# Moving the second block of attention values, a projection and the out-projections to other score tiles in a one-core AdaLN block

## The chip, the cores and the metric

The kernel runs on one core of one Trainium2 chip. The metric is the device time of one execution in microseconds. The matrix engine is called PE or TensorE here, with PEld for its weight loads; VectorE is DVE, ScalarE is ACT, GpSimd is POOL, and SP is the engine whose queue issues most of the DMAs.

## What is computed

A transformer block with adaptive layer norm, in float32. There are B = 2 sequences of S = 1024 positions with D = 256 features, H = 16 heads of 128, and a gated MLP with 704 hidden units whose weights come as integers with a scale per row.

```
sa, ca, ga, sb, cb, gb = six rows of silu(c) @ wmod, per sequence
ga, gb = sign(g) * max(|g|, 0.25)
h = layernorm(x) * (1 + ca) + sa
q, k, v = h @ Wq + bq, h @ Wk + bk, h @ Wv + bv         # 16 heads
q, k = rotary(q / sqrt(128)), rotary(k)
p = softmax(causal(q @ k.T));  x = x + ga * (concat(p @ v) @ Wo + bo)
h = layernorm(x) * (1 + cb) + sb
x = x + gb * ((silu(h @ Wgate.T) * (h @ Wup.T)) @ Wdown.T)
```

## The kernel before, in words

The work is a list of 32 units, one for each sequence and head, called heads here and counted from 0 (in the code `units`, and `n` is the number in the list). Each head has eight score tiles `i` = 0 to 7 of 128 queries. Every engine works its instructions off in the order in which the Python code issues them: a manual schedule writes that order out by hand, so the place of a call in the loop (L733 to L773) is the place of its instructions in every queue, DMAs included. Pools of PSUM banks and of SBUF buffers add the waits: a new tile in a pool waits until the oldest one in it has been read.

One step of the loop, for head `n` and tile `i`, issues in this order:

- `project_out` (L511): two matmul instructions (each float32 product is two instructions) of an earlier head's output tile with `Wo` into the one bank of `ps_y`, and on VectorE the product with 1/denominator added to `x` (L521). Heads n-1 (tiles 0 to 3, at i = 4 to 7) and n-2 (tiles 4 to 7, at i = 0 to 3) take turns.
- `score` (L419): q times k for the causal part of 128(i+1) keys into one of the two buffers of `ps_sc`, then on VectorE the mask and the row minimum (L434).
- `turned` (L461): for tile i-1 VectorE transposes the probabilities in 32x32 pieces (L465) into a staging tile; after tiles 3 and 7 sixteen DMAs on SP (L477) finish the transposition of a block of four tiles into `pT`. Tile 7 is turned in tile 0 of the next head. Each block has one `pT` buffer.
- `expo` (L446): the exponential on ScalarE (L451), with the row sum.
- `release` (L414): VectorE's part of the rotary embedding (L404) for the last q or k projection, and GpSimd's addition (L407).
- `project_qk` (L379): half of the next head's q or k into one of the two banks of `ps_a`, with two ScalarE copies (L400) and a GpSimd product (L401). It is called at i = 1, 3, 4 and 6.
- `values` (L481): p times v for one block of 512 queries into the one bank `po` of `ps_o`, then a copy of it on ScalarE (L500). The second block of the previous head is at i = 5 and 6, four key tiles each; the first block of the head itself at i = 7.
- `project_v` (L362) at i = 0 and 2, into `ps_a`, and the scattered work of `extras` (L629): weight scaling, layer-norm statistics, the bias row (L347) and the modulation (L117).

In the last head there is no next head to project, and `hidden` (L534) for the first half of sequence 0 takes that place at i = 0 to 5: gate and up products (L547), SiLU on ScalarE (L566, or L558 for the last, narrower chunk) and the product on VectorE (L567, L562). Behind the loop (L775 to L808) the remaining gate and up chunks alternate with the remaining out-projections, which take a bank in turn from `banks` (L502); then come the last values, layer norm, and the down products (L569).

Of the kernel before, what the change touches and what calls it, by code (L numbers as in the profile page):

```python
# [13 lines left out]
AF = mybir.ActivationFunctionType  # L14
ALU = mybir.AluOpType
# [5 lines left out]
HID = 704  # L21
NT = S // P
# [3 lines left out]
NF = (HID + P - 1) // P  # L26
FULL = (HID // P) * P
# [10 lines left out]
def adaln_block(ctx: ExitStack, tc: tile.TileContext, a, cos_d, sin_d, out):  # L38
    nc = tc.nc
# [7 lines left out]
    ps_a = pool("ps_a", 2, space=PSUM)  # L47
    ps_o = pool("ps_o", 1, space=PSUM)
    ps_y = pool("ps_y", 1, space=PSUM)
# [94 lines left out]
    pgs = []  # L144
# [211 lines left out]
    def add_bias(b, t):  # L356
        nc.gpsimd.tensor_tensor(x[b][:, t, :], x[b][:, t, :], gbo[b], ALU.add)
# [123 lines left out]
    def values(u, blk, k0, k1):  # L481
        b, g, h = u
        if blk == 0 and k0 == 0:
            outs[u] = opool.tile([P, S], F32, tag="o", name=f"o_{b}{g}{h}")
        if k0 == 0:
            pos[u, blk] = ps_o.tile([P, 512], F32, tag="o", name=f"po_{b}{g}{h}{blk}")
        po = pos[u, blk]
        last = 4 * blk + 3
        pT = pTs[u, blk].rearrange("p r i k b -> p i r k b")
        for k in range(k0, k1):  # L490
            off = max(0, k - 4 * blk)
            nc.tensor.matmul(  # L492
                po[:, off * P :],
                vs[b, g][:, k, ts(h, DH)],
                pT[:, off:, :, k, :],
                start=(k == 0),
                stop=(k == last),
            )
        if k1 == last + 1:
            nc.scalar.copy(outs[u][:, ts(blk, QB)], po)  # L500

    banks = [(ps_y, "y"), (ps_o, "o"), (ps_a, "a"), (ps_a, "a")]  # L502
    turn = [0]

    def bank(name):
# [5 lines left out]
    def project_out(u, t, late=False):  # L511

        b, g, h = u
        if t % 4 == 0:
            nc.vector.reciprocal(rdens[u][:, t : t + 4], dens[u][:, t : t + 4])  # L515
        name = f"py_{b}{g}{h}{t}"
        py = bank(name) if late else ps_y.tile([P, 512], F32, tag="y", name=name)
        nc.tensor.matmul(  # L518
            py[:, :D], outs[u][:, ts(t, P)], weights[b, g]["o"][:, h, :], start=True, stop=True
        )  # L520
        nc.vector.scalar_tensor_tensor(  # L521
            x[b][:, t, :], py[:, :D], rdens[u][:, t : t + 1], x[b][:, t, :], ALU.mult, ALU.add
        )


    h2s, gTs = {}, {}
# [4 lines left out]
        h2s[b, blk] = hpool.tile([P, KC, QB], F32, tag=tag, name=f"h2_{b}{blk}")  # L531
        return h2s[b, blk]

    def hidden(b, blk, c, late=True, first=None):  # L534
        if c == 0 if first is None else first:
            gTs[b, blk] = fpool.tile([P, NF, QB], F32, tag="f", name=f"gT_{b}{blk}")
        last = c == NF - 1
        if late:
            pg = ps_sc.tile([P, S], F32, tag="sc", name=f"pgu_{b}{blk}{c}")
            pgs = [pg[:, ts(j, QB)] for j in range(2)]  # L540
        else:
            pgs = [
                ps_a.tile([P, 512], F32, tag="a", name=f"pgu_{b}{blk}{c}{j}") for j in range(2 - last)
            ]
        for pg, n in zip(pgs, ("gate",) if last else ("gate", "up")):
            for k in range(KC):
                nc.tensor.matmul(  # L547
                    pg,
                    wT["last"][:, k, :] if last else wT[n][:, k, ts(c, P)],
                    h2s[b, blk][:, k, :],  # L550
                    start=(k == 0),
                    stop=(k == KC - 1),
                )
        sg = ppool.tile([P, QB], F32, tag="p", name=f"sg_{b}{blk}{c}")
        if last:

            m = HID - FULL
            nc.scalar.activation(sg[m:], pgs[0][:m], AF.Silu)  # L558

            for j, rows_ in enumerate((slice(0, m), slice(m, P))):  # L560
                part = lambda t: t.rearrange("p (t j q) -> p t j q", j=2, q=P)[:, :, j, :]
                nc.vector.tensor_tensor(  # L562
                    part(gTs[b, blk][rows_, c, :]), part(sg[m:]), part(pgs[0][m:]), ALU.mult
                )
        else:
            nc.scalar.activation(sg, pgs[0], AF.Silu)  # L566
            nc.vector.tensor_tensor(gTs[b, blk][:, c, :], sg, pgs[1], ALU.mult)  # L567

    def down(b, blk):  # L569

# [58 lines left out]
    def extras(n, i):  # L629

        if i == (2 if n else 7) and units[n][2] == 0:
            fold_out(*units[n][:2])
        if n == 1 and i == 0:
            modulation(2, ps_y, "y")
            shift_scale(2)

        if n == 2 and i == 7:
            ffn_scale_load()
        for m, name in ((3, "gate"), (5, "up"), (6, "last")):
            if n == m and i == 7:  # L640
                ffn_weight_load(name)
            if n == m + 1 and i in (2, 5):
                ffn_weight_scale(name, i // 4)
        if n in (0, 4, 6, 8) and i == 7:
            load_x(1, max(0, n - 2), 2, nc.scalar)
        if n == 7 and i == 7:
            ffn_down_load()
        if n in (8, 9) and i in (1, 3, 5):
            ffn_down_scale(n - 8, i - 1)


        for m, b, name in ((14, 1, "a"), (30, 0, "b")):

            j = i - 1 if n in (m - 5, m - 3) else i + 3
            if n in (m - 5, m - 4) and 1 <= i <= 4:
                ln_stats(b, name, j)
            if n == m - 4 and i == 6:
                ln_sqrt(b, name, 0, NT)
            if n in (m - 3, m - 2) and 2 <= i <= 5:
                ln_move(b, name, j - 1)  # L660
            if n in (m - 3, m - 2) and 1 <= i <= 4:
                ln_scale(b, name, j // 4, (j % 4,))
            if n in (m - 2, m - 1) and i == 6:
                ln_send(b, name, ((0, 1), (2, 3))[n - m + 2])
            if n == m and i in (4, 5, 7):
                blk = i // 6
                if i != 5:
                    dest = (new_hT if b else new_h2)(b, blk)
                else:
                    dest = (hT if b else h2s)[b, blk]  # L670
                for f in {4: (0,), 5: (1,), 7: (0, 1)}[i]:
                    ln_shift(b, name, blk, 0 if b else 2, dest, f)
        if n == 14 and i == 5:
            bias_row()
        if n == 15:
            add_bias(0, i)
        if n == 20:
            add_bias(1, i)

    with tc.manual_schedule():  # L680
        pc = ps_a.tile([P, 512], F32, tag="a", name="pc")
# [51 lines left out]
        for n, u in enumerate(units):  # L733
            b, g, h = u
            prev = units[n - 1] if n else None
            nxt = units[n + 1] if n + 1 < N else None
            nb, ng = (b, g + 1) if g + 1 < NG else (b + 1, 0)
            more = nb < B
            for i in range(NT):

                if i < 4 and n > 1:
                    project_out(units[n - 2], 4 + i)
                if i >= 4 and prev:
                    project_out(prev, i - 4)
                ps, nmax = score(u, i)
                if i >= 1:
                    turned(u, i - 1)
                elif prev:
                    turned(prev, NT - 1)
                expo(u, i, ps, nmax)  # L750
                release()
                if i in (1, 3, 4, 6) and nxt:
                    project_qk(nxt, *{1: ("q", 0), 3: ("k", 0), 4: ("q", 1), 6: ("k", 1)}[i])
                if i in (5, 6) and prev:
                    values(prev, 1, 4 * (i - 5), 4 * (i - 4))

                if i == 7 and prev:
                    values(u, 0, 0, 4)
                if i in (0, 2):
                    if h == 0:  # L760
                        project_v(b, g, 4 + i, *((ps_a, "a") if n else (ps_o, "o")))
                    elif more:
                        project_v(nb, ng, i)
                if n == 1 and i == 2:
                    values(prev, 0, 0, 4)
                if not nxt and i < NF:
                    hidden(0, 0, i, late=False)
                extras(n, i)
                if i == 7 and h == 1:
                    if more:  # L770
                        load_out(nb, ng)
                    if n + 3 < N:
                        load_proj(*units[n + 3][:2])  # L773

        u, prev = units[-1], units[-2]  # L775
        turned(u, 7)
        for c in range(4):
            hidden(0, 1, c)
            project_out(prev, 4 + c, late=True)
            project_out(u, c, late=True)  # L780

        for t in range(4):
            ln_stats(1, "b", t)
# [91 lines left out]
```

## Time and profile before

| what | us |
|---|---|
| median of three runs (lowest, highest) | 1077.45 (1077.07, 1077.51) |
| the profiled execution, its own time | 1076.87 |
| its span, from first to last instruction | 1075.1 |
| TensorE matmul busy | 1068.8 |
| VectorE busy | 656.8 |
| ScalarE busy | 507.2 |
| GpSimd busy | 397.1 |
| ScalarE waiting for VectorE's row minimum (L451 for L434) | 406.8 |
| VectorE waiting for the scores (L434 for L431) | 124.5 |
| SP's queue waiting for VectorE's transposes (L477 for L465) | 236.6 |

The granted TensorE clock is 1.000 over the whole span. Two more lines of the page show what the queue of SP carries:

```profile
pT<-t SPq DMA_DIRECT2D x512, 128.0 KB, 2.4
pT<-t SPq DMA_DIRECT2D x512, 64.0 KB, 2.0
```

The last column is the median time from issue to landing in us. In the trace these DMAs are issued some 0.63 us apart, so sixteen of them take about 10 us of the queue.

A group's row in the profile gives line, engine, operation, the tiles written and read, the shape and the count; behind the bar stand the busy time and the mean length of one in ns; behind the second bar the engine's idle time just before them, with what ended it. In a timeline or a chain the columns are the start in us from the span's beginning, the length in us, and what ran. Each line of the chain follows what released the step before it.

### The profile page before, as it was taken

How to read it: one execution, taken by the hardware profiler on the slowest of the kernel's cores; microseconds unless marked ns; L12 is line 12 of the kernel's file. 1: busy time of each engine (PE TensorE's matmuls, PEld its weight loads, DVE VectorE, ACT ScalarE, POOL GpSimd, SP SyncE). 2: the span in 40 equal slices, each digit the busy share in tenths (PEclk: the TensorE clock that was granted, in tenths of full speed). 3: DMA queues.
4: the chain of work that ended last, by engine and by line, in shares of the span. 5: the costliest groups of instructions: out<-in, count | busy, mean ns of one | idle time of the engine just before them, and what ended most of it. 6: DMA issues, size and time to landing. Idle time of an engine off the chain costs nothing.

```text
span 1075.1 us, 12365 instructions
## 1 busy us (share of the span) xinstructions
PE 1068.8 (99%) x3529; PEld 639.0 (59%) x3529; DVE 656.8 (61%) x1423; ACT 507.2 (47%) x956; POOL 397.1 (37%) x364
## 2 busy tenths in 40 slices
PE   9999999999999999999999999999999999999998
PEld 5655556566666656556566666656556566555656
DVE  5666566767767766556666566666667856444421
ACT  4644445445445544445455444544455455562110
POOL 4725353535344343664343444334343434200000
PEclk9999999999999999999999999999999999999999
DMA  6455655657554556556564645454655556423001
GB/s 218 109 133 123 161 138 128 172 126 182 117 145 99 140 119 152 126 130 144 111 147 108 147 107 138 95 143 103 157 118 120 143 130 141 104 52 66 20 20 39
DMA packets 66655, 130.97 MB, mean 122 GB/s; under 512 B 18806, under 2 KB 22010, under 8 KB 66588
## 3 DMA queue, kind: packets, MB, share of 16 engines
q1 hardware_dynamic: 64804, 125.78, 49.5%
q10 hardware_dynamic: 1736, 4.29, 1.2%
q8 instruction: 28, 0.46, 0.2%
q14 instruction: 39, 0.32, 0.1%
q0 software_dynamic: 48, 0.13, 0.1%
HBM read 25.26 MB, written 2.10 MB: 25 GB/s over the span
## 4 chain that ended last, share of the span: by engine, by line
PE 98%; DMA 1%; ACT 0%; issue 0%; DVE 0%; SPq 0%; DVEq 0%; ACTq 0%
PE po L492 23%; PE ps L431 23%; PE pv L370 10%; PE pq L388 10%; PE pk L388 10%; PE py L518 10%; PE pgu L547 7%; PE pd L592 3%; DMA wmod<-in_wmod 0%; PE pd L582 0%; PE pm L125 0%; PE ptx_a L218 0%; ACT L566 0%; DMA pT<-t 0%; PE pg L149 0%; PE ptx_b L218 0%
## 5 line engine op out<-in xcount | busy, mean ns | idle before, releaser
L451 ACT ACTIVATE p<-ps,nmax 128x128 f32<-128x128 f32 (+7 forms) x256 | 189.6, 741 | 407.6 <-DVE nmax L434 406.8
L431 PE MATMUL ps<-kT,qT 128*128 128x512 f32 (+3 forms) x768 | 289.4, 486 | 0.0
L434 DVE CUSTOM_DVE_ANT_0 ps<-ps,mask 128x128 f32<-128x128 f32 (+7 forms) x256 | 195.4, 763 | 125.2 <-PE ps L431 124.5
L492 PE MATMUL po<-pT,v 128*128 128x512 f32 (+3 forms) x768 | 263.8, 486 | 0.7 <-DMA pT<-t 0.5
L521 DVE SCALAR_TENSOR_TENSOR x<-py,rden,x 128x256 f32<-128x256 f32 x256 | 122.8, 482 | 183.8 <-PE py L518 176.1
L492 PEld LDWEIGHTS po<-pT,v 128*128 128x128 f32 x768 | 145.4, 190 | 130.6 <-issue 107.5
L465 DVE STREAM_TRANSPOSE t<-p 128x128 f32<-128x128 f32 (+7 forms) x256 | 198.0, 773 | 3.0 <-DMA pT<-t 2.1
L431 PEld LDWEIGHTS ps<-kT,qT 128*128 128x128 f32 x768 | 145.7, 190 | 77.5 <-issue 64.3
L401 POOL TENSOR_TENSOR r_k<-r_k,sin_t 128x512 f32<-128x512 f32 x64 | 81.3, 1271 | 221.6 <-ACT r_k L400 221.5
L518 PE MATMUL py<-wo,o 128*128 128x256 f32 x512 | 151.3, 379 | 0.0
L407 POOL TENSOR_TENSOR kT<-kT,r_k 128x512 f32<-128x512 f32 x64 | 81.2, 1269 | 138.7 <-DVE rden L515 117.4
L401 POOL TENSOR_TENSOR r_q<-r_q,sin_t 128x512 f32<-128x512 f32 x64 | 81.6, 1275 | 137.0 <-ACT r_q L400 134.9
L518 PEld LDWEIGHTS py<-wo,o 128*128 128x128 f32 x512 | 92.6, 190 | 65.1 <-issue 53.1
L370 PE MATMUL pv<-wv,hT 128*128 128x256 f32 x512 | 121.1, 379 | 0.0
L388 PE MATMUL pq<-hT,wq 128*128 128x512 f32 x256 | 120.5, 593 | 0.0
L388 PE MATMUL pk<-hT,wk 128*128 128x512 f32 x256 | 120.3, 592 | 0.0
L370 PEld LDWEIGHTS pv<-wv,hT 128*128 128x128 f32 x512 | 94.8, 190 | 19.5 <-issue 1.3
L400 ACT ACTIVATE r_q<-pq,cols 64x512 f32<-64x512 f32 x128 | 87.3, 682 | 22.5 <-PE pq L388 20.2
L407 POOL TENSOR_TENSOR qT<-qT,r_q 128x512 f32<-128x512 f32 x64 | 83.5, 1305 | 32.2 <-DVE qT L404 29.4
L400 ACT ACTIVATE r_k<-pk,cols 64x512 f32<-64x512 f32 x128 | 87.3, 682 | 6.1 <-PE pk L388 0.4
L388 PEld LDWEIGHTS pk<-hT,wk 128*128 128x128 f32 x256 | 48.6, 190 | 54.6 <-issue 44.7
L388 PEld LDWEIGHTS pq<-hT,wq 128*128 128x128 f32 x256 | 46.2, 190 | 33.1 <-issue 30.6
(96 smaller groups left out, 686.9 us busy)
## 6 DMA issues: line engine op xcount, KB each, us to landing
pT<-t SPq DMA_DIRECT2D x512, 128.0 KB, 2.4
pT<-t SPq DMA_DIRECT2D x512, 64.0 KB, 2.0
wq<-in_Wq SPq DMA_DIRECT2D x16, 256.0 KB, 3.0
wk<-in_Wk SPq DMA_DIRECT2D x16, 256.0 KB, 4.1
wv<-in_Wv SPq DMA_DIRECT2D x16, 256.0 KB, 4.1
wo<-in_Wo SPq DMA_DIRECT2D x16, 256.0 KB, 2.9
out<-yo SPq DMA_DIRECT2D x15, 128.0 KB, 1.8
wmod<-in_wmod SPq DMA_DIRECT2D x4, 256.0 KB, 5.7
```

The lines of the kernel that those rows point to most:

```text
L370: nc.tensor.matmul(pv[:, ts(j, HG * DH)], hT[b, n][:, k, ts(r, P)], weights[b, g]["v"][:, k, :], start=(k == 0), stop=(k == KC - 1),)
L388: nc.tensor.matmul(pq, weights[b, g][s][:, k, ts(h, DH)], hT[b, n][:, k, :], start=(k == 0), stop=(k == KC - 1),)
L400: nc.scalar.activation(r1[to], pq[of], AF.Identity, bias=cols[of, c : c + 1])
L401: nc.gpsimd.tensor_tensor(r1, r1, sin_t[:, sl], ALU.mult)
L407: nc.gpsimd.tensor_tensor(dst[:, sl], dst[:, sl], r1, ALU.add)
L431: nc.tensor.matmul(ps[:, c:e], qT[:, ts(i, P)], kT[:, c:e], start=True, stop=True)
L434: nc.vector.tensor_tensor_reduce(ps[:, :L], ps[:, :L], mask[:, NT - 1 - i :, :].rearrange("p t k -> p (t k)"), -SCALE, FLT_MAX, ALU.add, A ...
L451: nc.scalar.activation(p[:, :L], ps[:, :L], AF.Exp, bias=nmax, scale=-1.0, accum_out=dens[u][:, i : i + 1])
L465: nc.vector.transpose(t32[blk][:, :, j, : i + 1, :].rearrange("p c k b -> p k c b"), p[:, : (i + 1) * P].rearrange("p (k c a) -> p k c a", ...
L492: nc.tensor.matmul(po[:, off * P :], vs[b, g][:, k, ts(h, DH)], pT[:, off:, :, k, :], start=(k == 0), stop=(k == last),)
L518: nc.tensor.matmul(py[:, :D], outs[u][:, ts(t, P)], weights[b, g]["o"][:, h, :], start=True, stop=True)
L521: nc.vector.scalar_tensor_tensor(x[b][:, t, :], py[:, :D], rdens[u][:, t : t + 1], x[b][:, t, :], ALU.mult, ALU.add)
```

## The change

Nothing is added to the computation and nothing is taken from it. These calls move:

- `values` of the previous head's second block: from tiles 5 and 6 to tiles 6 and 7.
- `values` of the first block: from tile 7 of the head itself to tile 0 of the next head, after `project_v` (tile 2 in head 1, as before). For the last head it goes behind the loop.
- `project_qk` for the second half of k: from tile 6 to tile 5.
- `project_out`: every one a tile later, now by a running number `s`.
- `hidden` in the last head: at tiles 0, 1, 3, 4, 5, 6; its product on VectorE is held back (`owed`) until after the next `project_out`, also behind the loop.
- the second modulation from head 1, tile 0 to head 0, tile 7; the bias row in head 14 from tile 5 to tile 7; the order of `banks`.

```diff
-    banks = [(ps_y, "y"), (ps_o, "o"), (ps_a, "a"), (ps_a, "a")]
+    banks = [(ps_y, "y"), (ps_a, "a"), (ps_a, "a"), (ps_o, "o")]
...
-    def hidden(b, blk, c, late=True, first=None):
+    def hidden(b, blk, c, late=True, first=None, hold=False):
...
+        rest = (last_gate_up if last else full_gate_up)(b, blk, c, sg, pgs)
+        if hold:
+            owed.append(rest)
+        else:
+            rest()
...
+    def full_gate_up(b, blk, c, sg, pgs):
+        nc.scalar.activation(sg, pgs[0], AF.Silu)
+        return lambda: nc.vector.tensor_tensor(gTs[b, blk][:, c, :], sg, pgs[1], ALU.mult)
...
-        if n == 1 and i == 0:
+        if n == 0 and i == 7:
             modulation(2, ps_y, "y")
             shift_scale(2)
...
-        if n == 14 and i == 5:
+        if n == 14 and i == 7:
             bias_row()
...
+    filler = (0, 1, 3, 4, 5, 6)
+
+    def shared_out(s, late=False):
+        if s >= 0:
+            project_out(units[s // NT], s % NT, late)
...
-                if i < 4 and n > 1:
-                    project_out(units[n - 2], 4 + i)
-                if i >= 4 and prev:
-                    project_out(prev, i - 4)
+                shared_out(8 * n + i - 13)
+                if owed:
+                    owed.pop()()
...
-                if i in (1, 3, 4, 6) and nxt:
-                    project_qk(nxt, *{1: ("q", 0), 3: ("k", 0), 4: ("q", 1), 6: ("k", 1)}[i])
-                if i in (5, 6) and prev:
-                    values(prev, 1, 4 * (i - 5), 4 * (i - 4))
-
-                if i == 7 and prev:
-                    values(u, 0, 0, 4)
+                if i in (1, 3, 4, 5) and nxt:
+                    project_qk(nxt, *{1: ("q", 0), 3: ("k", 0), 4: ("q", 1), 5: ("k", 1)}[i])
+                if i in (6, 7) and prev:
+                    values(prev, 1, 4 * (i - 6), 4 * (i - 5))
...
-                if n == 1 and i == 2:
+                if not nxt and i in filler:
+                    hidden(0, 0, filler.index(i), late=False, hold=True)
+
+                if prev and i == (0 if n > 1 else 2):
                     values(prev, 0, 0, 4)
-                if not nxt and i < NF:
-                    hidden(0, 0, i, late=False)
...
-        u, prev = units[-1], units[-2]
+        u = units[-1]
         turned(u, 7)
+        s = 8 * N - 13
         for c in range(4):
-            hidden(0, 1, c)
-            project_out(prev, 4 + c, late=True)
-            project_out(u, c, late=True)
+            hidden(0, 1, c, hold=True)
+            if c == 0:
+                values(u, 0, 0, 4)
+            for _ in range(2 + (c == 3)):
+                shared_out(s, late=True)
+                s += 1
+            owed.pop()()
```

More of the change, by code (lines that the diff above doesn't have):

```diff
@@ L554, in hidden, with last_gate_up, rest @@
         sg = ppool.tile([P, QB], F32, tag="p", name=f"sg_{b}{blk}{c}")
-        if last:
-            m = HID - FULL
-            nc.scalar.activation(sg[m:], pgs[0][:m], AF.Silu)
+        rest = (last_gate_up if last else full_gate_up)(b, blk, c, sg, pgs)
[3 more added lines that the diff above has]
+            rest()
+    owed = []
+    def last_gate_up(b, blk, c, sg, pgs):
+        m = HID - FULL
+        nc.scalar.activation(sg[m:], pgs[0][:m], AF.Silu)
+        def rest():
             for j, rows_ in enumerate((slice(0, m), slice(m, P))):
@@ L564, in hidden @@
                 )
-        else:
-            nc.scalar.activation(sg, pgs[0], AF.Silu)
-            nc.vector.tensor_tensor(gTs[b, blk][:, c, :], sg, pgs[1], ALU.mult)
+        return rest
+    def full_gate_up(b, blk, c, sg, pgs):
+        nc.scalar.activation(sg, pgs[0], AF.Silu)
+        return lambda: nc.vector.tensor_tensor(gTs[b, blk][:, c, :], sg, pgs[1], ALU.mult)
     def down(b, blk):
```

## The prediction

> **What bounds the kernel now.** I read the page first, then the waits, then the chain of waits in stretches, then the timeline of TensorE around every place where the chain leaves TensorE. From the page:
>
> ```profile
> PE 1068.8 (99%) x3529; PEld 639.0 (59%) x3529; DVE 656.8 (61%) x1423; ACT 507.2 (47%) x956; POOL 397.1 (37%) x364
> ...
> PE 98%; DMA 1%; ACT 0%; issue 0%; DVE 0%; SPq 0%; DVEq 0%; ACTq 0%
> ...
> L431 PE MATMUL ps<-kT,qT 128*128 128x512 f32 (+3 forms) x768 | 289.4, 486 | 0.0
> ...
> L492 PE MATMUL po<-pT,v 128*128 128x512 f32 (+3 forms) x768 | 263.8, 486 | 0.7 <-DMA pT<-t 0.5
> ```
>
> TensorE is the bound: 98% of the chain that ended last. DVE is the next at 61%. A busy matmul row is modelled, so I checked it with distances: in the timeline the score of tile 0 of one head starts 29.27 us after that of the head before in 25 of the 29 intervals from head 2 on (heads are counted from 0; head 14's 29.70 holds the bias row's 0.43). The chain in one such head has no gap (columns: start, us, what):
>
> ```profile
> 411.12 0.43 PE py L518 x2
> 411.55 1.29 PE ps L431 x4
> 412.84 3.43 PE po L492 x8
> 416.27 0.43 PE py L518 x2
> 416.70 1.50 PE ps L431 x4
> 418.21 1.72 PE pk L388 x4
> 419.92 2.16 PE po L492 x8
> 422.08 0.43 PE py L518 x2
> 422.51 1.72 PE ps L431 x4
> 424.23 2.16 PE po L492 x8
> 426.39 0.43 PE py L518 x2
> 426.82 0.22 PE ps L431 x2
> 427.04 1.73 PE pv L370 x8
> ```
>
> These are tiles 5, 6, 7 and the start of tile 0; each start is the last start plus its length. Summed over a head: 8 out-projections at 0.43, scores of 0.22 + 0.43 + 0.65 + 0.86 + 1.08 + 1.29 + 1.50 + 1.72 = 7.75, six projections 10.34, values 7.75: 29.28 us, which is the interval. So a head can't be shortened by order; only the places where TensorE stands can. There are few. One of them, a head in which the second block's transposed probabilities land too late:
>
> ```profile
> 293.19 0.20 PE py L518
> 293.39 1.92 DMA pT<-t
> 295.31 0.10 issue
> 295.42 3.67 PE po L492 x8
> ```
>
> TensorE's timeline has the scores of this tile 5 at 293.45; with 1.29 they end at 294.74 and values start at 295.42: 0.68 lost. The same reading gives 0.21 at tile 5 near 588.96 (scores from 587.46), 0.35 at tile 7 of head 1 (scores from 69.81, values at 71.88), and in the last head 0.45, where gate and up wait for ScalarE's SiLU:
>
> ```profile
> 933.41 0.81 PE L431 MATMUL ps<-kT,qT 128*128 128x384 f32 x2
> ...
> 933.86 0.60 ACT L566 ACTIVATE sg<-pgu 128x512 f32<-128x512 f32 x1
> ...
> 934.51 1.98 PE L547 MATMUL pgu<-h,wgateT 128*128 128x512 f32 x4 [0.29 <-ACT sg L566]
> ```
>
> (933.41 + 0.65 = 934.06.) Together 1.69 us. After a standstill the first matmul also runs some 0.07 to 0.10 longer (values 3.67 instead of 3.43 for eight, with the 0.1 before); the odd intervals show it: 30.02 instead of 29.27 is 0.75, not 0.68. With that, and a head of 29.36, the pool is about 2.1 us of 1075.1. The rest of what is not TensorE is the start (a 5.06 us wait for modulation weights, until 6.83) and the tail behind the last matmul (2.8 us); the change touches neither.
>
> **The change part by part.** No matmul, activation or DMA is added or removed, and SP's queue keeps its order. So the sum is stalls removed less stalls made. New tile lengths, from the pieces above: 4.54, 2.58, 2.81, 3.01, 3.23, 3.44, 5.36, 4.31 (before: 2.38, 2.58, 2.81, 3.01, 3.23, 5.15, 5.81, 4.31); the same 29.28.
>
> *Second block of values to tiles 6 and 7.* It was needed 2.38+2.58+2.81+3.01+3.23+1.72 = 15.7 us into the head, now 19.6+1.9 = 21.5: 5.8 later, while its 16 DMAs still follow the transpose in tile 0. The stalls of 0.68 and 0.21, and head 29.36, go: 0.75 + 0.29 + 0.09 = 1.1 us with restarts. DVE's next writer of that staging tile comes 2.2 later too. The next DMA into this pT must await tile 7's values, but its own transpose is done 2.4 us into the next head anyway: SP waits for nothing new.
>
> *First block to the next head.* Its DMAs start with tile 4's transpose, 2.16 later in the head; it is needed 2.16 + 2.38 later: 2.4 us gained. Head 1's 0.35 + 0.07 goes. The pT of this block is next written in tile 4, its values end at 4.5 us: free.
>
> *The one PSUM bank of po* now passes from tile 7's values to tile 0's, with py, ps and pv between: 0.43+0.22+1.73 = 2.38 us. The copy that frees it stands behind tile 7's exponential on ScalarE. This is just what the first block's copy does in the trace before: bank full at 426.39, and
>
> ```profile
> 426.76 0.57 ACT L500 COPY o<-po 128x512 f32<-128x512 f32 x1
> ```
>
> ends at 427.33, against a need at 428.77. Slack 1.4 us, cost 0; with the square root's table switch in two heads, where that copy ran 340.13 to 340.70 behind values ending 338.31, the slack is 0. I take 0 to 0.2 for the two.
>
> *Fourth projection to tile 5.* Its bank is freed by VectorE's rotation of the third, at 410.82 to 411.53 in the trace, 1.3 before tile 5's scores end (412.84). Queued behind: ScalarE's pair (1.38 us) now in tile 6, before tile 6's exponential, whose input needs 1.93 + 1.15 us anyway; VectorE's second rotation in tile 6, the longest tile. VectorE's work in tile 5 ends about 0.8 into tile 6 and the scores there end at 1.9. Cost 0; heads with a weight scale of 0.88 in tile 5 end at 1.6, still covered.
>
> *Out-projections one tile on, bias row, modulation.* The copies precede the new places by as much as before. The bias row (0.43) and modulation's 16 matmuls (1.8) are in the chain wherever they stand. Head 0 now ends with modulation, and head 1's tile 1 scores need tile 7's exponential: by the rows (VectorE free of tile 6 near 43.0, then 1.15, then 1.11) that ends about 45.6, TensorE is there at 45.85. 0 to 0.2; I take 0.05.
>
> *Last head.* Gate and up go to tiles 0, 1, 3, 4, 5, 6 and the product is held until after the next out-projection. Between two of them lie py, scores and (tile 2) a whole tile. The chain on ScalarE is per chunk: load 1.28, exponential, load 1.28, SiLU 0.60. Here a rule speaks against: the Trainium skill, "ScalarE: Activation LUTs", section "What ACT_TABLE_LOAD costs", gives 1283 ns for the load and about 1380 ns of drain for every switch, 2.66 us in all. The row shows the 1.28 but no drain: load at 932.56, SiLU at 933.86, next load at 934.47. By the rule a chunk costs 2 x 2.66 + 0.9 + 0.6 = 6.8 us against tiles of 5.0 to 5.2, a stall of near 1.7 in each of three tiles, 5 us; by the row 4.1, and I take the row. Followed tile by tile, the 0.45 (0.55 with restart) goes, since tile 2 now gives ScalarE 2.4 us between chunks instead of 1.1; two exponentials in a row make the third SiLU end about 0.3 before it is needed; the fourth ends about 0.1 to 0.2 after the gate of the fifth could start. New stall 0 to 0.7, I take 0.25. Out-projections 1.08 apart at tile 2 just clear the single py bank (VectorE reads it 0.64 to 1.04 after its start).
>
> *Behind the last head.* Nine late out-projections instead of eight, the eighth on the bank of po, and values follow after one more of 0.43. The accumulation reads it 0.64 + 0.43 + 0.40 after the group starts, values could start at 1.29: 0.2, with restart 0.3. Bounds 0 to 0.5.
>
> **Sum.** Removed 0.75 + 0.29 + 0.09 + 0.42 + 0.55 = 2.1. Made 0.05 + 0.1 + 0.25 + 0.3 = 0.7. Net 1.4 us less. The profiled execution took 1076.87 with a span of 1075.1 (1.8 around it), so its like would take 1075.5 with a span of 1073.7; the median shown is 1077.45, 0.58 above the profiled one, and by the same difference I forecast 1076.05.
>
> **Rivals.** (1) Slower: the hand-over of the po bank binds in every head. Queue order speaks for it: the copy stands behind an exponential, which stands behind VectorE. If ScalarE's chain in tile 7 ran 1.6 us late (one displaced pair of 1.38 plus a wait), each of 31 heads would lose 0.2: 6.2 - 1.4, so 1082. It decides from 1.4 us of lateness on. Against it is the copy row above, measured behind the same exponential. (2) No change at all: each stall removed reappears in the last head and behind it, made stalls 2.1: 1077.4. For it speaks ScalarE's chain there, near 90% of a tile; against, that only two chunks are tight. (3) Everything goes and nothing comes: 1075.3; that is the floor, for there is no more to gain than 2.1 us.
>
> **Chances.** A measurement of this kernel can tell about 0.2% from no change, 2.15 us: 1075.3 and below is faster, 1079.6 and above slower. The forecast case (1075.4 to 1076.8) 0.62, rival 2 with its neighbourhood to 1079.6 0.19, rival 1 or another in-order queue that I misjudged 0.12, rival 3 0.07. Faster 0.07, same 0.81, slower 0.12. The range leaves out the slower case and the ends of the others: 1075.2 to 1078.0.
>
> **What would show it.** Right: tile 0 scores 29.27 apart in all heads but 14; no "DMA pT<-t" before po in TensorE's idle time; the po copy of tile 7 ending over 1 us before tile 0's values start; one short wait at values behind the last head, released by VectorE. Wrong: idle time of po released by ScalarE's copy in many heads, the fourth projection waiting for VectorE, or gate and up waiting over 0.5 for SiLU.

## The result and the profile after

| | before | after |
|---|---|---|
| median, us (lowest to highest, runs) | 1077.53 (1076.28 to 1079.76, 22) | 1075.98 (1075.21 to 1077.33, 22) |
| ratio, 95% interval | | 0.9986 [0.9980, 0.9992] |
| profiled execution, us | 1076.87 | 1076.84 |
| its span, us | 1075.1 | 1075.1 |
| first score of head 0 at, us | 24.03 | 25.11 |
| from there to the end of the span, us | 1051.07 | 1049.97 |

The changed kernel is 1.55 us shorter; 1076.05 was forecast, in a range of 1075.2 to 1078.0. A second timing, in another session, gave 1075.59 against 1077.81, ratio 0.9978 [0.9972, 0.9985].

The two profiled spans are equal, but the change is not without effect: the two executions differ in their start. The modulation shows it; this is its view of one tile in after, and then in before (columns: shortest/median/longest matmul in ns, first and last start in us):

```profile
L125 PE MATMUL pm<-sc,wmod x16: 421/421/551, 6.8 to 10.1; 128*128 128x128 f32 x16
```

```profile
L125 PE MATMUL pm<-sc,wmod x16: 273/273/347, 6.8 to 8.6; 128*128 128x128 f32 x16
```

The same 16 matmuls on the same data, which neither kernel changes, took 3.75 us in this execution of after and 2.02 in that of before. In two later profiles of after they took 2.02 again, and its head 0 began at 24.10 and 23.94. So I compare "the body", the time from the first score of head 0 to the end of the span: it is 1.10 us less in this pair. In the two later profiles of after it was 1049.96 and 1049.95.

The page of after:

```profile
PE 1070.5 (100%) x3529; PEld 641.4 (60%) x3529; DVE 655.1 (61%) x1423; ACT 507.7 (47%) x956; POOL 396.1 (37%) x364
...
PE 99%; DMA 0%; DVE 0%; SPq 0%; issue 0%
...
L492 PE MATMUL po<-pT,v 128*128 128x512 f32 (+3 forms) x768 | 263.7, 486 | 0.1
```

The same 3529 matmuls; TensorE's share of the chain went from 98 to 99%; the idle time of TensorE ahead of po (the product with the values) fell from 0.7 to 0.1 us, and "DMA pT<-t" as its releaser is gone. The scores of tile 0 are 29.27 us apart in every head from 2 on but three: 14 (29.70, bias row) and 11 and 27 (29.44). In those two ScalarE switches to the square root and back, and TensorE's wait is in the timeline of after (columns: start, us, engine, line, operation):

```profile
337.38 0.58 ACT L500 COPY o<-po 128x512 f32<-128x512 f32 x1
338.01 2.42 PE L492 MATMUL po<-pT,v 128*128 128x512 f32 x8
```

The copy out of the bank ends at 337.96 and the first block's values start at 338.01. In an ordinary head the copy ended at 219.58 and values started at 220.85: 1.27 us to spare, as in 25 of the 29 heads from 2 to 30 (the two others that are not 11 or 27 have 1.0 and 1.7).

The other waits that the change makes lie in the last head and behind it. The chain there:

```profile
943.45 0.43 PE py L518 x2
943.88 1.29 PE ps L431 x4
945.17 1.98 PE pgu L547 x4
...
978.73 0.45 PE py L518 x2
979.18 0.03 issue
979.20 0.93 DVE x L521 x2
980.13 0.04 issue
980.17 2.84 PE po L492 x6
```

Four gate matmuls take 1.72 (4 x 0.43); 1.98 holds 0.26 of waiting, at the fifth chunk of gate and up: the SiLU of the fourth ended at 945.11. Behind the last head TensorE has left the chain: values begin at 980.17 only when VectorE has read the out-projection that lay in po's bank. That is 0.41 us with the slower first matmul after a standstill, which I call the restart.

### The profile page after: what moved, and what is told of

It is laid out like the page before. It is cut to its first block, busy times and chain, and to the rows that moved or that the text cites. A ratio compares the mean times of both kernels' runs of the same rounds, so it can differ in the third digit from the quotient of the medians.

```text
span 1075.1 us, 12364 instructions
## 1 busy us (share of the span) xinstructions
PE 1070.5 (100%) x3529; PEld 641.4 (60%) x3529; DVE 655.1 (61%) x1423; ACT 507.7 (47%) x956; POOL 396.1 (37%) x364
## 4 chain that ended last, share of the span: by engine, by line
PE 99%; DMA 0%; DVE 0%; SPq 0%; issue 0%
PE po L492 23%; PE ps L431 23%; PE pv L370 10%; PE pq L388 10%; PE py L518 10%; PE pk L388 10%; PE pgu L547 7%; PE pd L606 3%; PE pm L125 1%; DMA wmod<-in_wmod 0%; PE pd L596 0%; PE ptx_a L218 0%; PE pg L149 0%; PE ptx_b L218 0%; PE pd_11r L606 0%; DVE x L521 0%
```

## The experiments

Bodies are 1051.07 before and 1049.97 after, unless another profile is named.

**The first block alone.** Before, with the first block of values in tile 0 of the next head; everything else as before.

```diff
-                if i == 7 and prev:
+                if i == 7 and not nxt:
                     values(u, 0, 0, 4)
...
-                if n == 1 and i == 2:
+                if prev and i == (0 if n > 1 else 2):
                     values(prev, 0, 0, 4)
```

> The kernel before with one move alone: the first block of values goes from tile 7 to tile 0 of the next head (for the last head it stays at tile 7). Theory A: tile 0 is then 2.16 us longer, so the second block at tiles 5 and 6 is also needed 2.16 us later than its head's start, against 0.7 us by which its data came late at most; all stalls on transposed probabilities go, the score of tile 0 is 29.27 us apart in all heads from 2 on but head 14, and from the first score of head 0 to the end of the span it takes 1051.07 - 0.42 - 0.75 - 0.29 - 0.09 = 1049.5. Rival: only the second block's own move to tiles 6 and 7 makes room; then the intervals of 30.02 and 29.56 stay and it takes 1050.65.

Measured: 1078.42 against 1077.99, ratio 1.0005 [0.9997, 1.0013]; body 1051.44. The stalls stayed, now in heads 15 and 24 (30.07 and 30.05). Its chain in head 15:

```profile
469.66 1.29 PE ps L431 x4
470.95 0.56 issue
471.50 3.67 PE po L492 x8
```

That is the picture of before's tile 5: 0.56 in which TensorE stands, then values of 3.67. My theory was wrong. Tile 7, 2.16 shorter, also lets the next head start earlier against its own transpose. Counted from the first score of a head, the second block's DMAs were first issued at 4.8 us instead of 2.6, and the last of them landed at 16.7 (median) instead of 14.5; TensorE was ready for values at 17.45 instead of 15.29. So the room between landing and need stayed 0.8 us, as before. It is the second block's own move that makes the room: in after the last DMA lands mostly at 13.9 to 15.7, at most at 18.2, against a need at 21.1. (The 15.7 and 21.5 of the prediction count from the out-projection, 0.43 earlier.)

The body is even 0.37 longer than before's first. Part of that is the last head, where values now stand ahead of the first gate: gate and up waited 0.85 for SiLU there, and 0.56 in before.

**The last head undone.** After, with gate and up in tiles 0 to 5 and no hold there.

```diff
-    filler = (0, 1, 3, 4, 5, 6)
+    filler = (0, 1, 2, 3, 4, 5)
...
-                    hidden(0, 0, filler.index(i), late=False, hold=True)
+                    hidden(0, 0, filler.index(i), late=False)
```

> The changed kernel with the last head as before: gate and up at tiles 0 to 5, each product issued at once. Theory A: the wait of 0.45 us for the SiLU with its restart (0.55) comes back at the third chunk, and the waits of the changed kernel in that head, 0.20 at the out-projection of tile 3 and 0.26 at the fifth chunk, go: 0.1 us slower than the changed kernel, so nothing that a median can tell. Rival: the last head was what the change is for and carries most of the 1.5 us between the medians: then 1 us slower.

Measured: 1075.79, ratio 0.9981 [0.9974, 0.9987], not told apart from after; body 1051.40. The body is longer only by a thing that has nothing to do with the edit: head 8 took 30.99, for the load of the scales was late in this execution.

```profile
247.08 8.22 DMA s_down<-in_scales
...
257.34 0.48 DVE x L521
257.82 0.04 issue
257.87 0.70 PE py L518 x2
```

VectorE waited 2.5 us for that load (0.2 to 2.5 in the ten profiles that have this wait) with the accumulation of an out-projection queued behind it. The last head itself was 0.28 us better than in after: 0.18 of waiting at one chunk where after has 0.26 at the fifth chunk and 0.20 at the out-projection of tile 3.

**The hand-over of po, with 0.65 us of cover left.** Cover means the matmuls between two uses of po's bank, 2.38 us in after. After, with values of the first block ahead of the v projection in tile 0.

```diff
+                if prev and i == 0 and n > 1:
+                    values(prev, 0, 0, 4)
...
-                if prev and i == (0 if n > 1 else 2):
+                if prev and i == 2 and n == 1:
                     values(prev, 0, 0, 4)
```

> The changed kernel with the first block of values ahead of project_v in tile 0, so that only 0.65 us of matmuls (py and ps) instead of 2.38 lie between the second block's last values and the next use of the po bank. Theory A: the bank is free 3.10 us after tile 7's scores end; it is now needed 2.16 + 0.65 = 2.81 after them; 0.34 with the semaphore and 0.1 of restart in each of 29 heads: 13 us slower, 1089, and the wait named is ScalarE's copy. Rival 1 of the prediction (ScalarE's queue runs over 1 us later than the row shows): over 1.4 us a head, over 40 us.

Measured: 1095.83 (one run); most heads 29.88, so 0.61 a head where 0.44 was expected; body 1070.38. The chain is that of rival 1:

```profile
99.90 1.21 ACT p L451 x2
101.11 0.48 ACT o L500
101.59 0.04 issue
101.64 2.42 PE po L492 x8
```

Exponential, copy, values: each begins as the one before it ends.

**No cover at all.** After, with the first block right behind the second in tile 7.

```diff
+                if i == 7 and prev:
+                    values(u, 0, 0, 4)
...
-                if prev and i == (0 if n > 1 else 2):
+                if n == 1 and i == 2:
                     values(prev, 0, 0, 4)
...
-            if c == 0:
-                values(u, 0, 0, 4)
```

> The changed kernel with the first block of values back in tile 7, right behind the second block's last four key tiles, with no matmul in between. Theory A: the bank is needed 2.16 us after tile 7's scores end and free at 3.15: 1.0 with 0.1 of restart in each of 30 heads, 33 us slower, about 1109. Together with the run that has 0.65 us in between it gives a line: each us of cover taken away beyond the slack of 1.4 costs 1 us a head. A rival in which the bank does not matter gives no change.

Measured: 1119.78 (one run); most heads 30.54, 1.27 each. Between these two runs, 0.65 us less cover cost 0.66 more a head. Carried back along that slope, after has 1.2 us to spare (its cover of 2.38, less the 0.65 of cover left here, less the 0.61 lost, plus the 0.1 of restart). The row gave 1.27.

**The fourth projection back.** After, with the second half of k in tile 6.

```diff
-                if i in (1, 3, 4, 5) and nxt:
-                    project_qk(nxt, *{1: ("q", 0), 3: ("k", 0), 4: ("q", 1), 5: ("k", 1)}[i])
+                if i in (1, 3, 4, 6) and nxt:
+                    project_qk(nxt, *{1: ("q", 0), 3: ("k", 0), 4: ("q", 1), 6: ("k", 1)}[i])
```

> The changed kernel with the fourth projection back at tile 6, so that tile 5 is 1.72 us long and tile 6 7.08. Theory A: its bank and its rotation have over 1 us of room in either place and the second block's values follow it in both: no change, 1049.97 from the first score of head 0 to the end of the span, within 0.2. Rival: VectorE's 3.1 us of work in a tile 5 of 1.72 us delays the row minimum of tile 6 and with it a score: then some tenths in every head, 5 us or more.

Measured: 1080.92 against 1078.42, ratio 1.0027 [1.0020, 1.0034]; body 1055.24, 5.3 longer. My "no change" was wrong, and the rival's 5 us came, but not from every head. All but 0.07 of it lies in eight heads where VectorE has a piece of layer norm to do by tile 5: 11, 27 and 28 lost 1.24 each, 12 lost 0.68, and 9, 10, 25 and 26 0.21 each. Head 11:

```profile
352.05 1.13 DVE xn_a L204
...
353.37 0.49 DVE x L521
353.86 0.04 issue
353.90 0.70 PE py L518 x2
```

The normalization stands in VectorE's queue ahead of the accumulation that frees py, and TensorE waits for it. Once the second block has left tile 5, that tile holds 1.72 us of TensorE's work; the projection makes it 3.44 and covers VectorE again.

**Both kernels again, unchanged.** One profile each.

> The kernel before, unchanged, for a second profile. Theory A: the waits for transposed probabilities come where SP's queue issues a DMA late while it loads its next 16 KB of instructions (in the first profile a late issue of 1.78 us at 283.9 and one of 1.59 at 583.0 stand ahead of the two waits, each at the time of an instruction load), and whether one of the 28 loads falls into the sixteen issues of a second block changes from run to run: the waits of 0.75 and 0.29 move to other heads or change in number, and each has a late issue ahead of it. Rival: they belong to heads 9 and 19 by the schedule (other DMAs there): then they stay there.

> The changed kernel, unchanged, for a second profile. Theory A: late issues are as many, but none makes TensorE wait, since the second block has 3 to 7 us of room: all heads 29.27 but 11 and 27 (29.44) and 14 (29.70), and 1049.97 from the first score of head 0 to the end of the span. The start is a second draw: the modulation's 16 matmuls took 3.75 us in the first profile of this kernel and 2.02 in all others; here either.

Measured: before, 1079.33 with a body of 1052.28; after, 1075.82 with 1049.96. After's intervals came out as in its first profile, head by head. Before's did not: its stalls were now in heads 8, 9, 12, 23 and 28 and small ones in 6 and 14 (29.38 to 30.07), none in 19, and none at tile 7 of head 1. What comes ahead of most of them is in SP's queue; first the issues, then a line on the DMA queues, of before's second profile from 694.5 to 697.6 us (the stall follows at 706.15; q8 is one of the queues that load instructions):

```profile
L477 SPq DMA_DIRECT2D pT<-t x3: 590/592/2079, 694.5 to 697.2; - x3
```

```profile
q8 instruction: 1, 0.02, 3.2%
```

An issue of pT takes SP 0.59 us, and 16 follow each other 0.63 apart. One of them took 2.08, and all behind it came 1.5 later. Beside it one packet of 0.02 MB passed on the queue that loads instructions, from 695.25 to 696.83; the issue ended at 697.20. The same pair stands ahead of the stall of 0.68 in before's first profile (an issue of 1.78 at 283.9). Three profiles have the second block in tile 5: before's two and that of the first block alone. In them eleven issues of over 1 us fell into a second block. The seven of 1.40 or more, so at least 0.81 late, were each followed by a stall of 0.3 to 0.8; the four of 1.31 or less, at most 0.72 late, by none. The room of 0.8 lies just between.

Not every stall has a late issue ahead of it. Head 8's (0.58) has none: its sixteen DMAs were issued on time, but landed 3.9 us after their issue (median) instead of 2.4. The first of them ran beside the load of the down weights (768 KB, landed at 254.57), as in before's first profile; why they caught up there and not here stays open. Nor has head 14's 0.08. And head 12's is there in all three profiles (29.36, 29.42 and 29.32): its fourteenth DMA is issued 0.3 late every time, in after too.

**A version without the made waits.** After, with the last head undone as above, but the scores of its tile 1 ahead of that tile's out-projection; the square root one tile earlier; the scaling's work two tiles later; the old order of banks.

```diff
-    banks = [(ps_y, "y"), (ps_a, "a"), (ps_a, "a"), (ps_o, "o")]
+    banks = [(ps_y, "y"), (ps_o, "o"), (ps_a, "a"), (ps_a, "a")]
...
-        if n in (8, 9) and i in (1, 3, 5):
-            ffn_down_scale(n - 8, i - 1)
+        if n in (8, 9) and i in (3, 5, 7):
+            ffn_down_scale(n - 8, i - 3)
...
-            if n == m - 4 and i == 6:
+            if n == m - 4 and i == 5:
...
```

> The changed kernel less its own waits: the last head's gate and up at tiles 0 to 5 with the product at once (0.46 of waits become 0.18), in its tile 1 the score ahead of the out-projection (the 0.18 goes too, since ScalarE's chain for the second chunk starts 0.43 earlier), the old order of banks (the 0.41 at values behind the last head goes), the square root's call at tile 5 instead of 6 (2 x 0.16), and the scaling of the down weights at tiles 3, 5, 7 instead of 1, 3, 5, so that VectorE does not wait for its scale's DMA. From the first score of head 0 to the end of the span: 1049.97 - 0.46 - 0.41 - 0.32 = 1048.8, so 1.2 us below the changed kernel, 2.7 below the one before. Rival: TensorE's waits that are taken away come back elsewhere in the last head; then 1049.5 or more.

Measured: 1075.01 (1074.58 to 1075.79), ratio 0.9966 [0.9955, 0.9977]; body 1049.26. Every head is 29.27 but 14. One wait is left, behind the last head:

```profile
963.63 0.59 ACT o L500
964.22 0.04 issue
964.27 0.70 PE py L518 x2
```

The old order gives the second late out-projection po's bank while ScalarE still copies out of it: 0.51. So the last run put po's bank third, beside after once more on the same chip.

```diff
+    banks = [(ps_y, "y"), (ps_a, "a"), (ps_o, "o"), (ps_a, "a")]
```

> The run with the changed kernel's waits taken out (e5_best), with the banks of the late out-projections in the order y, a, o, a. In e5_best one wait is left in front of the down products, 0.40 with 0.10 of restart at the second late out-projection: its bank is that of po, which ScalarE has just begun to copy. In the changed kernel the bank of po comes eighth of nine and values wait for it (0.31 and 0.10). In the third and seventh place neither should happen: the third is issued a chunk (3.43 us) later, and the seventh is read 1.04 us after the last three start, before values could (1.29). Theory A: no wait of TensorE from head 0 to the down products, 1049.26 - 0.51 = 1048.75 from the first score of head 0 to the end of the span, and 1074.5 as a median. Rival: the order does not matter and a wait of 0.4 comes in another place: 1049.2.

> The changed kernel, unchanged, on the same chip as e9_best_banks, for a direct comparison: 1.2 us slower than it, 1049.97 from the first score of head 0 to the end of the span, and 0.1 to 0.3% faster than the kernel before, as in the first result. The rival that the first result was the luck of one chip gives no difference to the kernel before.

Measured: this version 1074.25 (1074.09 to 1074.58), ratio 0.9964 [0.9951, 0.9978], body 1048.75; after 1075.59, ratio 0.9978 [0.9972, 0.9985], body 1049.95. The place of the last wait, in the chain of the best version:

```profile
961.56 2.16 PE po L492 x8
963.72 0.86 PE py L518 x4
964.58 2.58 PE pgu L547 x6
```

Each start is the last start plus its length. From head 0 to the down products TensorE no longer stands anywhere.

## Why the prediction was right

**The bound: right.** A head is 29.27 us in both kernels; the pool of some 2 us was all there was. The best version found has a body of 1048.75, 2.3 below before's first profile and 3.5 below its second: the pool differs from execution to execution.

**The second block: mechanism right, cause not seen.** The stalls of 0.68, 0.21 and 0.09 went, and the first block's move alone did not take such stalls away. But I took them as belonging to heads 9, 19 and 12. That is so of head 12 only. The two larger ones belong to the execution: before has 0.8 us of room in an ordinary head, and a late issue of SP, up to 1.5 us late, eats it wherever it falls. After has at least 21.1 - 18.4 = 2.7 (18.4 is the latest landing in its three profiles), more than that, and the three bodies agree to 0.02 us though 3, 5 and 4 late issues fell into second blocks. My 1.1 us for this step was a draw of one profile: in the second the stalls at tile 5 add up to 2.7. The 0.42 in head 1 was a draw too; an issue of 1.63 stood ahead of it, and the second profile had one of 1.11 there and no stall. Of the "5.8 later", 2.16 is the first block's leaving, which by itself gains nothing. That late issues cause the stalls rests on their coincidence in the profiles and on the step at 0.8 us of lateness; no run here changed when instructions are loaded.

**The first block and po's bank: right.** Cost 0 in ordinary heads, with room of 1.2 to 1.3 instead of 1.4. The two square roots cost 0.16 each, 0.32 in all, where I took 0.1 of at most 0.2: I had put the slack at 0, and it was just below.

**The fourth projection: number right, reason incomplete.** I asked only whether it would wait in tile 5, and not what happens to tile 5 without it. Alone, leaving it in tile 6 costs 5.3 us. This part of the change, which I costed at nothing, keeps the gain.

**The last head: half right.** The old 0.55 went and 0.26 came at the fifth chunk (0.25 taken). "Just clear" was wrong: the out-projection of tile 3 waits 0.20 for VectorE, which had read that of tile 2 only 1.11 after its start (at 933.45), not 1.04. And the gain wasn't the new tiles' own: with the gates as before it would have been larger by 0.28. The likely reason is the values in tile 0, which stand behind the first gate there and give ScalarE time; where they stood ahead of it (the first block alone), the wait was 0.85. That table switches cost their load and no drain held: in the last head of after eight of the loads start 0.02 behind ScalarE's previous instruction, and the next one follows a load by 0.01 unless it waits for VectorE.

**Behind the last head:** 0.41 for 0.3, inside its bounds.

**The sum.** Made waits were 0.32 + 0.20 + 0.26 + 0.41 = 1.19, where I took 0.7, a miss of 0.5. In the first pair of profiles the removed waits were 2.28: my 2.1 and two restarts that I had not listed, 0.07 in head 1 at 42.30 and 0.10 behind the last head at 961.36. The difference, 1.09, is the 1.10 by which the body fell. The median fell by 1.55, and by 2.22 in the second session, more than the body of this pair. That before's executions lose on average more to late issues than the one I read fits its second profile, but is not shown: medians hold the start too, and head 0 began between 23.59 and 25.11 in the profiles here. So that 1076.05 came within 0.1 of 1075.98 is luck; a made term too small and a removed term drawn from one execution cancel.

**Rival 1** (po's bank in every head) is real, and 1.2 us away: with 0.65 us of cover left, 1.73 less than in after, it cost 20 us (one run). **Rival 2** failed: the new waits took back 1.19 of the 2.28, not all. **Rival 3** (nothing new comes) is not what this change did, but the best version did it, and with 1074.25 went below the 1075.3 that I called the floor.

## What to carry to other kernels

Where one engine is at 98% and its work can't shrink, list the places where it stands and price the change by them alone; but profile the kernel before twice, for a stall that wanders from head to head is jitter that meets thin room, and what the change is worth is the room it makes. Before moving work out of a tile, ask what that work covered: the filler put in its place can be worth more than the move itself. Where one PSUM bank is copied out and filled again, keep enough other matmuls between (here some 1.2 us, and 2.4 in a head with a table switch), and look at which bank each step of a tail gets: that alone was worth 0.5 us here.

## What the runs showed of the hardware

Loads of instructions are not free for a queue that issues DMAs all the time. The queue q8 has 28 or 29 of them in a run, one every 37 us or so. Of 1024 issues of pT, 15 and 14 in before's two profiles and 9, 10 and 9 in after's took over 1 us instead of 0.59 (up to 2.1). In all twelve profiles there are 139 such issues, and 138 of them ended 0.2 to 0.4 us, mostly 0.37, after a load on q8 had ended. Whose instructions these are, no run shows. They are probably not SP's own: before's first trace has 28 loads, 1267 instructions of SP and 7364 matmuls and weight loads of TensorE, which is 45 and 263 for each load. The Trainium skill, "Runtime: NRT & Kernel Launch", section "Instruction fetch mechanics", has refills in blocks of 16 KiB, 256 instructions, fetched ahead, and the crossing "mostly hidden". The size agrees (16,384 bytes). For TensorE the loads are hidden in the best version, where it never stands between head 0 and the down products. For SP's issues they are not: in each of the first two profiles 19 loads fell while SP was issuing, and 17 of them in before and 13 in after went with an issue of over 0.7 us.

The start can run at a lower rate that the profile's clock doesn't show: 421 ns for a matmul of modulation instead of 273, with a clock of 1.00 given for both stretches (before's trace has no clock record ahead of 11.17 us), and head 0 a microsecond later. The Trainium skill, "TensorE: Matmul & The Clock Gate", section "Part 1: The HAM clock gate", calls the number of slow matmuls at the start variable from run to run; whether it is that gate, no run here shows.
